# A two-layer kernel on one core: the skip term as transposes, B turned by four transposes, and another order of issue

## The chip, the cores and the metric

The kernel runs on one core of a Trainium2 chip. The metric is the device time of one execution in microseconds (us); lower is better. A core has a matrix engine (PE, whose weight loads the profile lists as PEld), three vector-like engines (DVE, ACT, POOL), and a queue, SP, that issues most of the DMAs.

## The reference

The input x is 16 images of 64 x 64 positions with 128 channels. Layer 0 normalises it in groups and runs a two-dimensional recurrence over the positions; its result is added to x. Layer 1 normalises that again and runs a state-space layer (Mamba) over the 4096 positions of an image, once forwards and once backwards with the same weights; the sum of both is added. The kernel spends most of its time in layer 1. What one direction computes, with 256 inner channels and 16 states:

```python
xz = x @ in_w.T
xc, z = jnp.split(xz, 2, axis=-1)
xt = conv(xc, conv_w)                       # 4 taps, causal, per channel
xc = silu(xt + conv_b)
dbl = xc @ x_w.T
dt, Bm, Cm = split(dbl, [8, 24], axis=-1)
dt = softplus(dt @ dt_w.T + dt_b)
A = -exp(A_log)
dA = exp(dt[..., None] * A)
dBx = dt[..., None] * Bm[:, :, None, :] * xc[..., None]
# for each position t:   h = dA_t * h + dBx_t;   y_t = sum over states of h * C_t
y = ys + xc * D
y = y * silu(z)
return y @ out_w.T
```

The change is about two places: `xc * D`, the skip term, and the way in which `Bm` reaches the product `dBx`.

## The kernel before

**Passes.** Layer 1 treats an image as 16 passes of 512 positions: passes 0 to 7 forwards, 8 to 15 backwards (`second` in the code). A pass holds two halves (h = 0 and 1) of 128 channels each, so a tile is 128 channels by 512 positions. There are 256 passes. During passes 0 and 1 of an image the next image is read as well, in eight pieces (`read_load`, `read_turn`, `read_take`, `read_stats`), and its group norm is worked out (`normal`). The tile for these loads, `xl`, exists once: a load waits until the piece before has been turned.

**One pass.** PE makes the convolution (`conv`, L1125), ACT `silu` of it, giving `xc`. PE projects it (`xproj`, L1162), and `dbl` holds the rows for dt, B and C. `dtproj` and `softplus` give `dt`; `times` on POOL gives `dtx` = dt * xc. For each of 16 states and both halves ACT makes `decay` (L1254), the tile `da` = exp(dt * A), and DVE runs a `scan` (L1308) over the positions: 32 scans a pass.

**States by two ways.** Four of the states (the units `0` and `1` of ORDER) get their input from POOL: `drive` (L1262) multiplies `dtx` with rows of B that were spread over the partitions (`br`). Their output is turned by PE (`turned`, L1340), taken by ACT (`turned_take`, L1348) and weighed with C on PE (`weigh`, L1355). The other twelve states (units `a` to `f`, four states each) get their input from PE: `drive_rows` (L1288) multiplies the transposed `dtx` (`turn`, L1242, and `turn_take`) with a matrix `d` that holds B on diagonals, and fills a quad of four PSUM banks (`hps`), which exists once. DVE scans from there; POOL multiplies two states with C (`out_of`, L1331, from `hst` and spread rows `cr` to `hc`), and PE adds them up with transposes into the output `py` (`sums`, L1368 through the helper `add`).

**The way of B.** `bturn` (L1182) turns `dbl` on PE, ACT takes it (`bturn_take`, L1193), SP writes it to a diagonal in DRAM (`scatter`, L1271, one DMA for four states), and loads the whole matrix from there (`spread`, L1207). The `scatter` of kind k does the same for C of the first four states straight from the rows in DRAM (L1278).

**Skip.** `ddiag` holds D on a diagonal, for each half. `skip` multiplies four blocks of `xc` with it on PE (L1368 through `add`), as the first contribution to `py`; `sums`, `weigh` and, backwards, `again` (the forward result, loaded by `recall`) add to it. Backwards follow `finish` on DVE, `back`, `back_take`, `project` and the store; `gate` and `gate_take` make silu(z) for that. Forwards, ACT's `finish` and a `spill` end the pass.

**The order.** Nothing in the kernel is ordered by hand. `order_of_issue` lists all operations with engine, dependences and buffers, and `simulate` plays them with assumed durations (COST, ISSUE, LINK) and an urgency for each kind of operation (URGENCY, a table for each direction); among the operations that are ready, the one with the lowest urgency is issued first. What comes out is the fixed order of instructions on each engine. RINGS gives the number of buffers of each kind; AHEAD and LEAD say how far the decays of the first four states may run ahead.

Of the kernel before, what the change touches and what calls it, by code (L numbers as in the profile page):

```python
# [8 lines left out]
F32 = mybir.dt.float32  # L9
# [5 lines left out]
P = 128  # L15
# [29 lines left out]
def units_of(order):  # L45

    count = {}
    for x in order:
# [4 lines left out]
        else:  # L53
# [6 lines left out]
    "br": 2, "cr": 6, "bt": 2, "xc": 5, "dt": 4, "dtx": 3, "dtxt": 3, "dbl": 2, "z": 1, "y": 1,  # L60
# [5 lines left out]
    "bturn": 0.5, "bturn_take": 0.23, "xproj": 1.0, "xproj_take": 0.4, "times": 1.2,  # L66
    "turn": 0.47, "turn_take": 0.555, "decay": 0.68, "drive": 2.4, "drive_rows": 1.13,
    "scan": 1.21, "keep": 0.6, "keep_group": 0.57, "out": 2.39, "sums": 0.88, "skip": 0.89,
# [3 lines left out]
    "read_take": 0.56, "read_stats": 0.69, "normal": 3.0, "normalise": 0.75, "spread": 0.6, "rows": 0.81,  # L72
# [10 lines left out]
AHEAD = 3  # L83
# [3 lines left out]
ISSUE = {"b": 0.7, "c": 0.7, "d": 0.51, "k": 0.45, "scatter_d": 0.82, "scatter_k": 1.77}  # L87
# [3 lines left out]
        {(0, 0): 226.07, (0, 1): 225.5, (0, 2): 209.71, (0, 3): 245.13, (1, 0): -224.93, (1, 1): -215.88,  # L91
         (1, 2): -217.49, (1, 3): -219.71},
        {(0, 0): 240.75, (0, 1): 97.67, (0, 2): 239.83, (0, 3): 183.31, (1, 0): -224.93, (1, 1): -236.77,
         (1, 2): -236.93, (1, 3): -239.63},
    ),
    "xproj": (
        {(): -4.49},
        {(): 88.92},
    ),
    "xproj_take": (  # L100
        {(): 12.43},
        {(): -21.38},
    ),
    "rows": (
        {(): -45.24},
        {(): -121.72},
    ),
    "bturn": (
        {(): 244.05},
        {(): -26.43},  # L110
    ),
    "bturn_take": (
        {(): 158.86},
        {(): 159.8},
    ),
    "dtproj": (
        {(0,): -250, (1,): -53.81},
        {(0,): 50.32, (1,): 50.35},
    ),
    "times": (  # L120
        {(0,): -65.05, (1,): -67.57},
        {(0,): 244.56, (1,): -165.67},
    ),
    "turn": (
        {(0,): 249.76, (1,): -134.89},
        {(0,): 229.21, (1,): 221.57},
    ),
    "turn_take": (
        {(0,): 47.45, (1,): 47.51},
        {(0,): 227.25, (1,): 226.2},  # L130
    ),
    "skip": (
        {(0,): 103.25, (1,): 218.48},
        {(0,): 89.87, (1,): 208.37},
    ),
    "spread": (
        {("b", 0): 48.09, ("d", 0): 223.16, ("c", 0): 189.13, ("c", 1): 239.27, ("d", 1): -105.98, ("c",
         2): 8.58, ("c", 3): 235.49, ("b", 1): 201.1, ("d", 2): 56.35, ("c", 4): 230.23, ("c", 5):
         215.44, ("k", 0): 139.69},
        {("b", 0): -14.32, ("d", 0): 47.86, ("c", 0): -35.94, ("c", 1): 138.92, ("d", 1): -107.61, ("c",  # L140
         2): -218.83, ("c", 3): -181.78, ("b", 1): -3.62, ("d", 2): 122.62, ("c", 4): 54.73, ("c", 5):
         240.7, ("k", 0): 139.45},
    ),
    "drive": (
        {(0, 0): -56.91, (1, 0): -57.77, (0, 1): 215.02, (1, 1): 247.85},
        {(0, 0): 171.33, (1, 0): 123.34, (0, 1): 160.79, (1, 1): 118.53},
    ),
    "decay": (
        {(0, 0): 224.88, (4, 0): 226.48, (5, 0): 240.06, (6, 0): 188.37, (7, 0): 250, (1, 0): 113.5, (8,
         0): 247.75, (9, 0): 250, (10, 0): 249.7, (11, 0): 249.33, (2, 0): 123.95, (12, 0): 249.4, (13,  # L150
         0): 176, (14, 0): 177.57, (15, 0): 243.29, (3, 0): 220.69, (4, 1): 238.79, (5, 1): 203.28, (6,
         1): 109.72, (7, 1): 15.19, (0, 1): 44.93, (8, 1): 223.62, (9, 1): 223.58, (10, 1): 225.51, (11,
         1): 223.77, (1, 1): 148.26, (12, 1): 223.35, (13, 1): 66.54, (14, 1): 65.52, (15, 1): 156.31,
         (2, 1): 205.76, (3, 1): 245.25},
        {(0, 0): 114.51, (4, 0): 225.16, (5, 0): 225.14, (6, 0): 226.99, (7, 0): 226.82, (1, 0): 116.2,
         (8, 0): 248.06, (9, 0): -17.84, (10, 0): -182.05, (11, 0): 70.11, (2, 0): 180.88, (12, 0):
         152.1, (13, 0): 166.91, (14, 0): 113.63, (15, 0): 222.06, (3, 0): 31.92, (4, 1): 221.8, (5, 1):
         236.29, (6, 1): 241.63, (7, 1): 222.65, (0, 1): 243.59, (8, 1): 198.45, (9, 1): 228.52, (10, 1):
         31.86, (11, 1): 26.36, (1, 1): 192.12, (12, 1): 244.33, (13, 1): 245.68, (14, 1): 241.41, (15,
         1): 243.62, (2, 1): 241.76, (3, 1): 250},  # L160
    ),
    "scan": (
        {(0, 0): -110.99, (4, 0): -110.09, (5, 0): -105.1, (6, 0): -105.34, (7, 0): -105.61, (1, 0):
         181.32, (8, 0): 19.6, (9, 0): 19.21, (10, 0): -80.71, (11, 0): 7.49, (2, 0): 40.13, (12, 0):
         -108.17, (13, 0): -102.34, (14, 0): -10.85, (15, 0): -108.25, (3, 0): -48.47, (4, 1): -48.83,
         (5, 1): -68.91, (6, 1): -83.82, (7, 1): -96.92, (0, 1): -31.74, (8, 1): -33.58, (9, 1): -38.05,
         (10, 1): -40.96, (11, 1): -50.07, (1, 1): 200.94, (12, 1): -50.19, (13, 1): -87.76, (14, 1):
         -88.26, (15, 1): -91.09, (2, 1): -5.51, (3, 1): -86.39},
        {(0, 0): -109.51, (4, 0): -109.17, (5, 0): -109.22, (6, 0): 181.52, (7, 0): 181.62, (1, 0):
         181.29, (8, 0): 178.29, (9, 0): 89.91, (10, 0): 53.07, (11, 0): 78.05, (2, 0): 236.4, (12, 0):  # L170
         238.58, (13, 0): 235.96, (14, 0): 231.8, (15, 0): 185.76, (3, 0): 215.03, (4, 1): -224.25, (5,
         1): -76.4, (6, 1): -164.06, (7, 1): -249.08, (0, 1): -59.15, (8, 1): 43.77, (9, 1): 17.69, (10,
         1): -44.01, (11, 1): 39.93, (1, 1): 179.06, (12, 1): 225.25, (13, 1): 220.27, (14, 1): 219.29,
         (15, 1): 208.64, (2, 1): 205.77, (3, 1): -93.1},
    ),
    "scatter": (
        {("d", 0): -144.33, ("d", 1): 131.97, ("d", 2): -55.93, ("k", 0): 242},
        {("d", 0): 229.49, ("d", 1): 250, ("d", 2): -140.49, ("k", 0): 202.88},
    ),
    "drive_rows": (  # L180
        {(0, 0): 146.61, (1, 0): 105.78, (2, 0): 191.69, (0, 1): 31.86, (1, 1): 23.35, (2, 1): 216},
        {(0, 0): 117.29, (1, 0): -235.5, (2, 0): -209.5, (0, 1): -218.03, (1, 1): -1.36, (2, 1): 220.27},
    ),
    "keep": (
        {(0, 0): 243.5, (1, 0): 34.18, (2, 0): 129.78, (3, 0): -79.15, (4, 0): 159.92, (5, 0): -249.25,
         (0, 1): 66.3, (1, 1): 176.21, (2, 1): 144.92, (3, 1): -209.94, (4, 1): 140.89, (5, 1): 96.84},
        {(0, 0): -158.59, (1, 0): 220.66, (2, 0): 74.58, (3, 0): -133.66, (4, 0): 174.52, (5, 0): 249.16,
         (0, 1): -179.84, (1, 1): -6.05, (2, 1): -230.81, (3, 1): -175.76, (4, 1): -72.61, (5, 1): 0.64},
    ),
    "out_of": (  # L190
        {(0, 0): 108.7, (1, 0): -34.28, (2, 0): -83.46, (3, 0): 208.24, (4, 0): 161.27, (5, 0): -58.6,
         (0, 1): 206.6, (1, 1): -49.46, (2, 1): -49.85, (3, 1): -249.28, (4, 1): -201.46, (5, 1): 30.29},
        {(0, 0): 70.5, (1, 0): -63.47, (2, 0): -69.72, (3, 0): 41.7, (4, 0): 117.41, (5, 0): 29.34, (0,
         1): -114.11, (1, 1): -106.56, (2, 1): -250, (3, 1): -250, (4, 1): -242, (5, 1): -12.92},
    ),
    "sums": (
        {(0, 0): 211.83, (1, 0): 214.79, (2, 0): 204.06, (3, 0): -118.64, (4, 0): 34.31, (5, 0): -162.93,
         (0, 1): 232.47, (1, 1): 221.1, (2, 1): 203.91, (3, 1): 184.07, (4, 1): -222.45, (5, 1): -216.44},
        {(0, 0): -193.31, (1, 0): -194.97, (2, 0): -209.87, (3, 0): -189.32, (4, 0): -201.67, (5, 0):
         -91.54, (0, 1): 250, (1, 1): 236.49, (2, 1): 104.24, (3, 1): 225.82, (4, 1): 240.77, (5, 1):  # L200
         166.95},
    ),
    "keep_group": (
        {(0, 0): 208.79, (0, 1): -155.94},
        {(0, 0): -223.05, (0, 1): -200.24},
    ),
    "turned": (
        {(0, 0, 0): -242.59, (0, 0, 1): 198.86, (0, 0, 2): -19.69, (0, 0, 3): -164.84, (0, 1, 0): 211.89,
         (0, 1, 1): -221.33, (0, 1, 2): -221.83, (0, 1, 3): -131.66},
        {(0, 0, 0): -224.04, (0, 0, 1): 147.65, (0, 0, 2): -245.55, (0, 0, 3): -163.35, (0, 1, 0):  # L210
         142.63, (0, 1, 1): 126.52, (0, 1, 2): 128.31, (0, 1, 3): 130.7},
    ),
    "turned_take": (
        {(0, 0, 0): 63.6, (0, 0, 1): 44.72, (0, 0, 2): 65.41, (0, 0, 3): 65.32, (0, 1, 0): -184.53, (0,
         1, 1): 128.22, (0, 1, 2): 127.61, (0, 1, 3): 106.49},
        {(0, 0, 0): 55.23, (0, 0, 1): 9.13, (0, 0, 2): 192.65, (0, 0, 3): 192.3, (0, 1, 0): -181.41, (0,
         1, 1): -222.89, (0, 1, 2): 132.46, (0, 1, 3): 131.21},
    ),
    "weigh": (
        {(0, 0): -231.65, (0, 1): -206.75},  # L220
        {(0, 0): -4.68, (0, 1): 4.67},
    ),
# [1276 lines left out]
```

## Time and profile before

| | |
|---|---|
| median of three runs | 12566.69 us (12562.89 to 12603.51) |
| the profiled execution | 12569.44 us, span 12567.3 us |
| mean granted clock of PE | 0.992 |
| busy: PE, DVE, POOL, ACT | 96%, 89%, 84%, 79% |
| POOL `hc` (out_of) | 7384.9 us in 3072 instructions, 2431 ns each |
| DVE `hst` scans with carry | 6466.2 us in 5376, 1261 ns each |
| ACT `da` (decay) | 5404.7 us in 8192, 710 ns each |
| PE `py<-ddiag,xc` (skip) | 580.2 us in 4096 records, 285 ns each |

Busy time is that in which an engine has at least one instruction under way. PE's instructions overlap, so the mean duration of one is longer than the distance from one to the next; what an operation on PE costs is read from the start of the next one. The profile names an operation by its line and its tiles, out<-in. "Idle before" gives the time for which the engine stood and what it waited for. The first pass of layer 1 begins 1538 us into the span.

### The profile page before, as it was taken

How to read it: one execution, taken by the hardware profiler on the slowest of the kernel's cores; microseconds unless marked ns; L12 is line 12 of the kernel's file. 1: busy time of each engine (PE TensorE's matmuls, PEld its weight loads, DVE VectorE, ACT ScalarE, POOL GpSimd, SP SyncE). 2: the span in 40 equal slices, each digit the busy share in tenths (PEclk: the TensorE clock that was granted, in tenths of full speed). 3: DMA queues.
4: the chain of work that ended last, by engine and by line, in shares of the span. 5: the costliest groups of instructions: out<-in, count | busy, mean ns of one | idle time of the engine just before them, and what ended most of it. 6: DMA issues, size and time to landing. Idle time of an engine off the chain costs nothing. (4 is left out here: it accounts for less than half of the span.)

```text
span 12567.3 us, 322625 instructions
## 1 busy us (share of the span) xinstructions
PE 12114.5 (96%) x128820; PEld 9486.8 (75%) x128820; DVE 11138.3 (89%) x11409; ACT 9954.8 (79%) x15936; POOL 10578.2 (84%) x4868
## 2 busy tenths in 40 slices
PE   9999999999999999999999999999999999999999
PEld 8656877777777777777777777777777777777777
DVE  7767699998989999999999998999999999999998
ACT  3444588888888888888888888888888888888887
POOL 0111299999999999999999999999999999999998
PEclk9999899999999999999999999999999999999999
DMA  4222255555556555555555555555555555556564
GB/s 156 56 56 56 64 162 160 158 166 158 160 157 166 159 160 158 165 160 158 167 159 162 158 163 161 162 163 158 162 158 163 159 163 161 162 159 165 158 164 140
DMA packets 2320782, 1885.92 MB, mean 150 GB/s; under 512 B 1537696, under 2 KB 1883312, under 8 KB 2319280
## 3 DMA queue, kind: packets, MB, share of 16 engines
q1 hardware_dynamic: 2241328, 1830.04, 52.2%
q10 hardware_dynamic: 77952, 35.24, 1.2%
q8 instruction: 1017, 16.66, 0.5%
q14 instruction: 485, 3.97, 0.1%
HBM read 1698.25 MB, written 164.30 MB: 148 GB/s over the span
## 5 line engine op out<-in xcount | busy, mean ns | idle before, releaser
L1331 POOL TENSOR_TENSOR hc<-hst,cr 128x1024 f32<-128x1024 f32 x3072 | 7384.9, 2431 | 465.0 <-DVE hst L1308 307.3
L1308 DVE TENSOR_TENSOR_SCAN hst<-da,carry,hps 128x512 f32<-128x512 f32 x5376 | 6466.2, 1261 | 535.0 <-issue 219.7
L1254 ACT ACTIVATE da<-dt,A_log_sb 128x512 f32<-128x512 f32 x8192 | 5404.7, 710 | 843.3 <-DVE hst L1308 783.9
L1368 PEld LDWEIGHTS py<-ident,hc 128*128 128x128 f32 x24576 | 2763.6, 142 | 769.0 <-issue 358.3
L1368 PE MATMUL py<-ident,hc 128*128 128x128 f32 x24576 | 3108.0, 275 | 165.7 <-POOL hc L1331 154.5
L1262 POOL TENSOR_TENSOR group<-dtx,br 128x1024 f32<-128x1024 f32 x1024 | 2447.0, 2403 | 134.8 <-PE ptg L1340 85.8
L1308 DVE TENSOR_TENSOR_SCAN group<-da,carry,group 128x512 f32<-128x512 f32 x1792 | 2243.8, 1266 | 118.9 <-ACT da L1254 108.3
L1288 PEld LDWEIGHTS hps<-d,dtxt 32*128 32x128 f32 x49152 | 1526.0, 187 | 621.8 <-issue 280.3
L1125 PE MATMUL pp<-xT,wk 128*128 128x512 f32 x4096 | 1954.8, 599 | 1.7 <-ACT dt L1229 1.2
L1288 PE MATMUL hps<-d,dtxt 32*128 32x128 f32 x49152 | 1810.0, 283 | 139.4 <-DVE hst L1308 117.3
L1348 ACT COPY ht<-ptg 128x512 f32<-128x512 f32 x2048 | 1126.9, 588 | 430.6 <-PE ptg L1340 398.9
L887 POOL TENSOR_TENSOR a_f<-a_f,c 128x16 f32<-128x16 f32 (+35 forms) x254 | 188.6, 743 | 1313.9 <-ACT a_f L879 1250.2
L1340 PE MATMUL ptg<-ident,group 128*128 128x128 f32 x8192 | 1153.0, 278 | 35.4 <-DVE group L1308 18.5
L1340 PEld LDWEIGHTS ptg<-ident,group 128*128 128x128 f32 x8192 | 922.4, 142 | 256.9 <-issue 91.9
L1125 PEld LDWEIGHTS pp<-xT,wk 128*128 128x128 f32 x4096 | 697.5, 190 | 524.9 <-issue 496.1
L1308 DVE TENSOR_TENSOR_SCAN hst<-da,hps 128x512 f32<-128x512 f32 x768 | 874.6, 1199 | 83.8 <-PE hps L1288 46.4
L1235 POOL TENSOR_TENSOR dtx<-dt,xc 128x512 f32<-128x512 f32 x512 | 646.8, 1288 | 61.6 <-DMA d<-d 29.5
L1254 ACT ACT_TABLE_LOAD x527 | 676.1, 1283 | 9.4
L1368 PE MATMUL py<-ddiag,xc 128*128 128x128 f32 x4096 | 580.2, 285 | 13.3 <-ACT y L1415 10.8
L1355 PE MATMUL py<-ht,k 128*32 128x128 f32 x16384 | 559.8, 277 | 2.6 <-ACT ht L1348 1.2
L879 ACT ACTIVATE a_f<-pg_f,b_sb 128x16 f32<-128x16 f32 (+35 forms) x508 | 219.7, 472 | 415.2 <-DMA x<-xl 212.7
L1368 PEld LDWEIGHTS py<-ddiag,xc 128*128 128x128 f32 x4096 | 496.2, 191 | 59.3 <-ACT y L1415 25.4
(113 smaller groups left out, 12431.2 us busy)
## 6 DMA issues: line engine op xcount, KB each, us to landing
cr<-rows SPq DMA_DIRECT2D x1536, 512.0 KB
d<-d SPq DMA_DIRECT2D x768, 448.0 KB
br<-rows SPq DMA_DIRECT2D x512, 512.0 KB
k<-k SPq DMA_DIRECT2D x256, 256.0 KB
yf<-y SPq DMA_DIRECT2D x128, 512.0 KB
yl<-yf SPq DMA_DIRECT2D x128, 512.0 KB
carry<-hst SPq DMA_DIRECT2D x3072, 1.0 KB
xs<-in_x_dram SPq DMA_DIRECT2D x64, 512.0 KB
```

The source lines that it names most:

```text
L879: nc.scalar.activation(agv.rearrange("p i b -> p (i b)"), pgv, AF.Tanh if g == "c" else AF.Sigmoid, bias=b_sb[:, gi : gi + 1],)
L1125: nc.tensor.matmul(self.ps["conv", h], lhsT=wk[:, k, h * P : (h + 1) * P], rhs=xT[self.b % 2][:, t0 : t0 + T], start=(k == 0), stop=(k == ...
L1235: nc.gpsimd.tensor_mul(self.dtx[h], self.dt[h], self.xc[h])
L1254: nc.scalar.activation(t, self.dt[h], AF.Exp, scale=amat[:, h, s : s + 1])
L1262: nc.gpsimd.tensor_mul(both[:, m : m + 2, :], bc(self.dtx[h], 1, 2), self.brow[q])
L1288: nc.tensor.matmul(part[:, j, :, :], lhsT=self.dtxt[h][rows, j, :], rhs=dg[rows, j + r, :, :], start=True, stop=True, skip_group_check=True,)
L1308: nc.vector.tensor_tensor_scan(t[:, self.rev], self.da.pop((s, h))[:, self.rev], dbx[:, self.rev], 0.0 if self.first else carry[:, self.d, ...
L1331: nc.gpsimd.tensor_mul(self.hc[g, h], self.hst[g, h].rearrange("p t m -> p m t"), self.crow[g])
L1340: nc.tensor.transpose(pt[:, k, :], self.group[g, h][:, t0 : t0 + TB, :].rearrange("p t s -> p (t s)"), ident,)
L1348: nc.scalar.copy(t, self.ps.pop(("turned", g, h, j)))
L1355: nc.tensor.matmul(self.py[h][q * TB : (q + 1) * TB, j * P : (j + 1) * P], lhsT=cd[:, GX * j + q, :], rhs=self.ht[g, h, j][:, q, :], start ...
L1368: nc.tensor.matmul(self.py[h][:, cols], **{"start": False, "stop": False, **how}, skip_group_check=True)
```

## The change

It does four things.

- `skip` no longer multiplies with `ddiag`. A new operation `scaled` on ACT multiplies `xc` by D (a factor for each partition), into a new tile `xd` with two buffers, and `skip` adds `xd` to `py` by four transposes. `ddiag` goes.
- `bturn` uses four transposes of all 128 partitions onto 64, in place of eight matmuls of 64x64; `bturn_take` copies 96 elements on 64 partitions instead of 48 on 128. The two halves of the positions lie side by side then, and `scatter` of kind d writes each by a DMA of its own: two issues for four states instead of one.
- `dtx` has two buffers instead of three.
- COST, ISSUE, AHEAD and the whole table URGENCY have other values, so the order of instructions on every engine is another one. The order of the scans on DVE stays the same but for the finishes and statistics between them.

```diff
-    "br": 2, "cr": 6, "bt": 2, "xc": 5, "dt": 4, "dtx": 3, "dtxt": 3, ...
+    "br": 2, "cr": 6, "bt": 2, "xc": 5, "xd": 2, "dt": 4, "dtx": 2, "dtxt": 3, ...
...
-AHEAD = 3
+AHEAD = 0
...
-ISSUE = {"b": 0.7, "c": 0.7, "d": 0.51, "k": 0.45, "scatter_d": 0.82, "scatter_k": 1.77}
+ISSUE = {"b": 0.45, "c": 0.44, "d": 0.46, "k": 0.34, "scatter_d": 1.2, "scatter_k": 0.65}
...
         for h in range(NH):
-            put("skip", (h,), "PE", after=[("silu", i, h)], takes=[py[h]], uses=[T_["xc"][h]], chain=("skip", 0))
+            xd = tile_of("xd")
+            put("scaled", (h,), "ACT", after=[("silu", i, h)], takes=[xd], uses=[T_["xc"][h]], chain=("scaled", 0))
+            put("skip", (h,), "PE", after=[get(("scaled", i, h))], takes=[py[h]], uses=[xd, T_["xc"][h]], chain=("skip", 0))
...
-            for h in range(NH):
-                nc.vector.tensor_scalar_mul(ddiag[:, h, :], ident, dvec[:, h, :])
...
-                pt = self.ps["bturn"] = bank(place, f"pbt_{self.nm}", (P, NB, QP))
+                pt = self.ps["bturn"] = bank(place, f"pbt_{self.nm}", (QP, NB, P))
                 strided = self.dbl.rearrange("p (i j) -> p j i", j=NB)
                 for j in range(NB):
-                    for q in range(NQ):
-                        part = slice(q * QP, (q + 1) * QP)
-                        nc.tensor.matmul(
-                            pt[part, j, :],
-                            lhsT=strided[part, j, :],
-                            rhs=ident[part, part],
-                            ...
-                        )
+                    nc.tensor.transpose(pt[:, j, :], strided[:, j, :], ident)
...
             def bturn_take(self):
-                self.bt = ring(cp, "bt", [P, NB, NS - NX], f"bt_{self.nm}")
-                nc.scalar.copy(self.bt, self.ps.pop("bturn")[:, :, RANK + NX : RANK + NS])
+                self.bt = ring(cp, "bt", [QP, NB, NQ, NS - NX], f"bt_{self.nm}")
+                pt = self.ps.pop("bturn").rearrange("p j (q s) -> p j q s", q=NQ)
+                nc.scalar.copy(self.bt, pt[:, :, :, RANK + NX : RANK + NS])
...
                 if kind == "d":
-                    dst = bass.AP(t.tensor, t.offset, [[WD + GX, P], [P, NB], [1, GX]])
-                    nc.sync.dma_start(dst, self.bt[:, :, GX * g : GX * (g + 1)])
+                    for q in range(NQ):
+                        dst = bass.AP(
+                            t.tensor, t.offset + q * QP * (WD + GX), [[WD + GX, QP], [P, NB], [1, GX]]
+                        )
+                        nc.sync.dma_start(dst, self.bt[:, :, q, GX * g : GX * (g + 1)])
                     return
...
+            def scaled(self, h):
+                self.xd[h] = ring(cp, "xd", [P, T], f"xd_{self.nm}_{h}")
+                nc.scalar.activation(self.xd[h], self.xc[h], AF.Copy, scale=dvec[:, h, :])
+
             def skip(self, h):
 
                 for j in range(NB):
                     self.add(
                         h,
                         slice(j * P, (j + 1) * P),
-                        lhsT=self.xc[h][:, j * P : (j + 1) * P],
-                        rhs=ddiag[:, h, :],
+                        lhsT=self.xd[h][:, j * P : (j + 1) * P],
+                        rhs=ident,
+                        is_transpose=True,
                     )
```

What the new order does at the places that matter below, told from the two programs' instructions. In pass 1 of an image, read_turn(4) on PE stood between the last `turned` and the `weigh` of the pass before; now it stands behind `drive_rows(2,0)`, and read_turn(3), (5), (6) and (7) lie between other operations than they did. The three small matmuls of `normal` stood ahead of that pass's `drive_rows(2,1)` and now stand behind it. In passes 3 to 7, `times(1)` and `turn(1)`, issued in the pass before until now, come in the pass itself, after its third scan. On SP, in passes 3 to 7, the issue behind the scatter of kind k is the spread of the next pass's first `cr`; before, it was mostly a `keep` or a d scatter.

## The prediction

> **What bounds the kernel now.** I read the page's busy shares first. They do not decide: four engines are above 79%.
>
> ```profile
> PE 12114.5 (96%) x128820; PEld 9486.8 (75%) x128820; DVE 11138.3 (89%) x11409; ACT 9954.8 (79%) x15936; POOL 10578.2 (84%) x4868
> ```
>
> So I cut the seventh image (counting from 0) at the first scan of each of its sixteen passes, in the view of busy time by window. The columns are the window, its length, then busy us and instructions of PE, PEld, DVE, ACT and POOL, the granted clock, the DMA share and GB/s. The passes shown are 0, 1, 2, 5, 8, 10 and 11.
>
> ```profile
> 6363.20:6408.50 45.30, 44.30 (x498) 34.85 (x498) 39.57 (x38) 39.65 (x62) 42.71 (x20) 1.00 0.55 160
> 6408.50:6460.10 51.60, 46.30 (x489) 38.00 (x487) 42.42 (x43) 43.17 (x68) 42.01 (x19) 0.90 0.64 173
> 6460.10:6500.30 40.20, 37.61 (x456) 29.23 (x449) 38.12 (x32) 36.99 (x58) 35.85 (x17) 1.00 0.48 133
> ...
> 6581.50:6622.20 40.70, 38.55 (x457) 30.12 (x456) 38.09 (x34) 34.71 (x54) 40.54 (x19) 1.00 0.59 156
> ...
> 6704.10:6746.30 42.20, 40.41 (x469) 31.96 (x468) 37.29 (x35) 33.54 (x53) 41.94 (x19) 1.00 0.62 172
> ...
> 6790.40:6834.10 43.70, 43.66 (x493) 34.89 (x492) 40.38 (x37) 36.36 (x58) 40.68 (x19) 1.00 0.57 159
> 6834.10:6877.80 43.70, 43.66 (x493) 34.88 (x492) 40.35 (x37) 36.34 (x58) 40.69 (x19) 1.00 0.57 164
> ```
>
> Three regimes show. In passes 9 to 15 PE is busy 43.66 of 43.70 us while every other engine idles 3 us or more: PE alone sets the time. In passes 3 to 8 POOL is busy all but 0.2 to 0.4 us of about 41: POOL sets it. Passes 0 and 1 hold the next image's reading; pass 1 leaves every engine idle for 5 us or more and has a clock of 0.90.
>
> Next the timeline of PE in such a PE-bound pass (start, length, engine, line, what).
>
> ```profile
> 6263.12 1.17 PE L1182 MATMUL pbt<-ident,dbl 64*64 64x64 f32 x16
> 6264.22 0.75 PE L1242 MATMUL ptx<-ident,dtx 128*128 128x128 f32 x4
> 6264.90 1.08 PE L1355 MATMUL py<-ht,k 128*32 128x128 f32 x32
> ...
> 6267.69 1.16 PE L1368 MATMUL py<-ddiag,xc 128*128 128x128 f32 x8
> 6268.69 0.60 PE L1423 MATMUL pb<-ident,y 128*128 128x128 f32 x4
> 6269.13 1.04 PE L1368 MATMUL py<-ident,hc 128*128 128x128 f32 x8
> ```
>
> No wait stands at any line, and an operation costs the distance to the next start: bturn 1.10 us, this skip 1.00, four plain transposes (pb) 0.44. The records also show that a matmul is two records and a transpose one: skip's four make x8, bturn's eight x16, pb's four x4. Last, the same view in pass 1:
>
> ```profile
> 6415.47 0.63 PE L1049 MATMUL pt<-ident,xl 128*128 128x128 f32 x4 [1.83 <-DMA xl<-x]
> 6416.03 1.57 PE L1355 MATMUL py<-ht,k 128*32 128x128 f32 x32
> 6417.53 2.09 PE L1288 MATMUL hps<-d,dtxt 32*128 32x128 f32 x32
> ...
> 6447.63 0.56 PE L736 MATMUL pm_l<-mv,gavg 128*128 128x1 f32 x2
> 6448.12 2.09 PE L1288 MATMUL hps<-d,dtxt 32*128 32x128 f32 x32
> ```
>
> Here a read_turn waits for its load, and drive_rows (hps) runs 2.09 us instead of 1.17 behind it; later it stands behind the three matmuls of the group norm.
>
> **The change on PE.** Skip: in that pass the first takes 0.89 us (start 6240.73 to 6241.62) and the second 1.00, together 1.89. The new ones are four transposes each with the same shape as pb and ptg, which take 0.44 (pb above) to 0.50 (pb from 6240.23 to 6240.73). Two cost 0.88 to 1.00, so 0.89 to 1.01 goes; I take 0.95. Bturn: four transposes read with a stride, onto 64 partitions. No row shows that. The nearest are pb's 0.44 and turn's 0.68 (ptx, strided, twice the columns). Against 1.10 that saves 0.42 to 0.66; I take 0.55, nearer the plain one because each load is half turn's. Together 1.31 to 1.67 us a pass, taken as 1.50: PE's need in passes 9 to 15 falls from 43.66 to 42.16.
>
> **Does the time follow?** POOL's 40.7 us there leaves room. DVE is tighter. Each quad of PSUM is freed by a scan, refilled by PE and read again, so DVE has idle time that it can't avoid. Pass 2 shows how much: neither POOL (idle 4.35) nor PE (2.59) is the bound there, and DVE idles 40.20 − 38.12 = 2.08. With DVE's 40.35 this gives 42.43, just above PE's 42.16. I take 42.5, from 43.76 on the mean of passes 9 to 15: 1.25 × 7 × 16 images = 140 us. The bounds are 1.6 (PE's whole saving, 180 us) and 0.75 (hand-offs worse than in pass 2, 84 us). Passes 2 to 8 are POOL's or the hand-off's: nothing.
>
> **Passes 0 and 1.** Pass 0 is PE's too (44.30 of 45.30): 1.2 us × 15 images = 18. In pass 1 the new order puts read_turn(4) behind weigh, two drive_rows, skip, two sums and four conv after read_turn(3): about 1.0 + 2.2 + 0.5 + 1.7 + 3.4 = 8.8 us of PE work. The load needed 4.95 from issue (6410.52 on SP) to use, so the 1.83 and the 0.24 wait before it go. The group norm's three matmuls now follow drive_rows(2,1); before, that one was free to start at 6446.0 and started at 6448.1: 2.1 us. With PE's own 1.5 that is 5.7. But between read_turn(4) and (5), and (6) and (7), stand only some 4.7 and 4.1 us of PE work against 4.95: I give back 2.2. ACT, busy 43.17 of 51.6, keeps room. 3.5 × 15 = 52 us; bounds 0 and 5.7 × 15 = 86.
>
> **What is added.** Two scaled activations of 128x512 on ACT: 11 decays of that size take 6.85 us in a row, 0.62 each, so 1.24; skip, which now waits for ACT, comes about 30 scans behind its scaled, for both h. ACT goes from 36.3 to 37.6 of 42.5, and its 5 us of idle hide them; what is queued behind one is a decay, whose tiles are up to 9 ahead. If that cover were gone, 1.24 × 7 × 16 = 139 us would come back. bturn_take grows from 48 to 96 elements: 0.20 us to at most the 0.37 of dbl's 256; take 0.03, hidden likewise. The dtx ring of 2 moves times(1) and turn(1) of passes 3 to 7 behind the pass's third scan; they are needed at drive(0,1) and drive_rows(0,1), some ten scans later, so nothing waits. ddiag's two products at the start: under 1 us.
>
> Each d scatter becomes two issues on SP: 3 more a pass, 0.50 us each (the median of the old ones), 1.5 us beside some 20 us of issuing in 43. What is queued behind them is the cr and d spreads, which are used ten us and more after their issue, and the keeps, which the next pass needs: nothing; the other bound is the 3.4 us which the issue behind k's scatter takes now, 3 × 3.4 a pass, still under SP's waiting. [...]
>
> **Sum.** 140 + 18 + 52 = 210 us. The profiled execution took 12569.4 (span 12567.3), 2.7 above the median of three runs, 12566.7. So 12569.4 − 210 = 12359, or 12356 beside the median.
>
> **Rivals.** (1) The hand-offs hold more than pass 2 shows, 43.0 a pass, and pass 1 gains nothing: 84 + 18 = 102, 12,465. For it: PE, DVE and POOL are then within 2 us of each other. Against: pass 2's row. 0.11.
>
> (2) More: passes 9 to 15 reach PE's 42.16 (180), and pass 1 gains all (86 + 22 in pass 0): 12,280. For it: PE waits 0.04 us a pass now. 0.07.
>
> (3) Half clock. Transposes replace matmuls, and if they keep the clock up less, PE slows in the passes which it sets. One spell like those in pass 1 costs about 2 us (2.09 − 1.17 for drive_rows, as much again in its neighbours); one in every PE-bound pass is 2 × 7 × 16 = 224: 12,580, no change. Against: passes 9 to 15 are full of transposes and show 1.00. [...] 0.05.
>
> (4) Slower: the SP queue starves POOL. Behind k's scatter the next issue takes about 3.4 us on SP (138 d scatters stood there, median 3.38). In passes 3 to 7 the new order puts a cr spread there, and three more issues follow. POOL multiplies with cr, and in passes 2 to 8 each us it waits is lost. It decides from 1.9 us of POOL waiting in each (250 / (8 × 16)); with the full 3.4 in eight passes, 3.4 × 128 = 435 − 210 = 225 slower, 12,790. For it: POOL waited 52.5 us for cr in 8000 before, so the margin isn't endless. Against: in the trace its buffer comes free 28.9 us into the pass and is first used 7.4 us into the next, some 19 us later. 0.11.
>
> **Numbers.** The forecast, 12,300 to 12,430, has 0.66. The range 12,240 to 12,520 takes in rivals 1 and 2 as well (0.84). About 0.3%, 38 us, is what a measurement of this kernel can tell from no change. Faster: 0.66 + 0.11 + 0.07 = 0.84, less a little for a rival 1 that falls shorter, 0.82; same 0.06; slower 0.12.
>
> **What would show it.** Right: windows of passes 9 to 15 at 42.2 to 42.9 with PE idle under 0.8, skip's start distances at 0.44 to 0.50, bturn's at 0.44 to 0.68, passes 3 to 8 unchanged with POOL idle under 0.8, pass 1 without a wait of 1.8 on xl before weigh. Wrong: a PE wait on ACT xd, POOL waits on cr in passes 3 to 8, a clock below 1.00 in passes 9 to 15, or PE's need above 42.5.

## The result, and the profile after

The changed kernel took 12487.88 us (median of four runs, 12473.08 to 12499.37) against 12577.49 for the kernel before in the same comparison: a ratio of 0.9926, with a 95% interval of 0.9903 to 0.9949. It is faster by 0.7%, where the prediction said 1.7%. The profiled execution took 12473.08 us, its span 12471.1.

The busy shares of the page again decide nothing:

```profile
PE 11816.2 (95%) x123700; PEld 9141.1 (73%) x123700; DVE 11102.2 (89%) x11407; ACT 10217.3 (82%) x16448; POOL 10573.6 (85%) x4868
```

Busy time by window, cut at the first scan of each pass of the seventh image, as before (window, length, then PE, PEld, DVE, ACT and POOL busy, granted clock, DMA share, GB/s). Shown are passes 0, 1, 2, 3, 5, 8 and 11:

```profile
6322.80:6365.60 42.80, 41.47 (x481) 33.17 (x480) 39.64 (x39) 38.75 (x63) 42.68 (x20) 1.00 0.60 171
6365.60:6415.40 49.80, 43.04 (x474) 33.95 (x473) 42.13 (x42) 45.37 (x72) 42.48 (x19) 0.95 0.66 183
6415.40:6456.90 41.50, 36.52 (x421) 28.04 (x420) 38.18 (x32) 38.34 (x60) 37.65 (x17) 0.95 0.50 130
6456.90:6501.10 44.20, 38.11 (x438) 29.83 (x439) 38.16 (x33) 35.76 (x56) 41.72 (x19) 0.96 0.49 148
...
6543.20:6584.80 41.60, 37.95 (x444) 29.19 (x444) 38.14 (x34) 35.79 (x56) 40.04 (x19) 1.00 0.58 161
...
6666.70:6707.70 41.00, 37.91 (x438) 29.00 (x436) 36.98 (x35) 33.72 (x53) 40.10 (x19) 1.00 0.54 159
...
6793.10:6835.50 42.40, 42.40 (x477) 33.32 (x473) 39.98 (x37) 37.40 (x59) 40.67 (x19) 1.00 0.56 165
```

The PE-bound pass 11 is 1.3 us shorter, with PE busy for all of it. But pass 3 has 44.20 us in which no engine is busy for more than 41.72, and the clock is 0.95 to 0.96 in passes 2 and 3. Pass 3 of before had a clock of 1.00, and POOL was busy for nearly all of it:

```profile
6500.30:6541.40 41.10, 38.92 (x458) 30.29 (x458) 38.21 (x33) 34.78 (x54) 40.92 (x19) 1.00 0.57 155
```

One image is too few to judge by, so here is each pass as a mean over images 1 to 15 (the distance from the first scan of a pass to the first of the next, read from the traces):

| pass | before | after | change |
|---|---|---|---|
| 0 | 45.26 | 42.65 | −2.61 |
| 1 | 49.63 | 49.03 | −0.60 |
| 2, 3, 4, 5 | 40.43, 41.04, 40.93, 40.91 | 42.11, 42.58, 42.54, 42.76 | +1.68, +1.54, +1.61, +1.85 |
| 6, 7, 8 | 41.20, 41.24, 41.79 | 41.31, 40.22, 41.54 | +0.11, −1.02, −0.25 |
| 9 to 15, mean | 43.76 | 42.46 | −1.30 |

Passes 9 to 15 give 1.30 × 7 × 16 = 146 us, and passes 2 to 6 take back 6.79 × 16 = 109. Passes 0, 1, 7 and 8 together give 4.48 × 16 = 72, about the 70 that was forecast for passes 0 and 1. So passes 2 to 6 are where the missing gain went.

Where PE is the bound, its timeline shows the new operations at their forecast pitch: bturn (`pbt`) 0.57 us to the next start, skip (`xd`) 0.44.

```profile
6824.16 0.64 PE L1182 MATMUL pbt<-ident,dbl 128*64 128x128 f32 x4
6824.73 0.72 PE L1236 MATMUL ptx<-ident,dtx 128*128 128x128 f32 x4
...
6828.66 0.60 PE L1365 MATMUL py<-ident,xd 128*128 128x128 f32 x4
6829.10 1.15 PE L1365 MATMUL py<-ident,hc 128*128 128x128 f32 x9
```

Now the lost time, in pass 3. The timeline of DVE, with the idle time before a group and its releaser in brackets:

```profile
6490.20 2.45 DVE L1305 TENSOR_TENSOR_SCAN hst<-da,carry,hps 128x512 f32<-128x512 f32 x2 [0.17 <-issue]
6496.41 2.45 DVE L1305 TENSOR_TENSOR_SCAN hst<-da,carry,hps 128x512 f32<-128x512 f32 x2 [3.76 <-DMA carry<-hst]
```

The scan that starts at 6496.41 is scan(14,1). It writes an `hst` buffer, of which there are three, and the DMA carry<-hst that it waits for is keep(2,1), which still reads the buffer that it needs. The timeline of SP's queue says why this 1 KB arrives so late:

```profile
6483.82 0.60 SPq L1275 DMA_DIRECT2D k<-rows  x1
6484.51 1.33 SPq L1207 DMA_DIRECT2D cr<-rows  x1
6485.93 0.38 SPq L1201 DMA_DIRECT2D d<-d  x1
6486.41 0.38 SPq L1207 DMA_DIRECT2D cr<-rows  x1
6486.91 2.25 SPq L1317 DMA_DIRECT2D carry<-hst  x1
```

The keep is the fifth issue, behind the scatter of kind k and three loads of 512, 448 and 512 KB for the next pass. It is issued at 6486.91 and the scan is released at 6496.41, 9.5 us later. In pass 3 of before only two loads, of 448 and 512 KB, stood ahead of it:

```profile
6526.42 1.01 SPq L1198 DMA_DIRECT2D rows<-dbl  x2
6527.52 0.37 SPq L1207 DMA_DIRECT2D d<-d  x1
6528.99 0.34 SPq L1213 DMA_DIRECT2D cr<-rows  x1
6529.44 0.59 SPq L1278 DMA_DIRECT2D k<-rows  x1
6530.11 3.79 SPq L1320 DMA_DIRECT2D carry<-hst  x1
```

On the mean of passes 3 to 5 the keep is issued 0.4 to 0.5 us after the scan whose result it copies, so it isn't issued late; it lands late, 7.9 to 8.1 us after its issue, where before it was 5.8 to 6.0 (from the landing events of the traces).

While DVE waits, PE has no quad to read or refill, and it starts again at about half its speed. The granted clock is 1.00 over the 2.74 us of matmuls ahead of the wait, 0.56 over the 1.92 us of drive_rows behind it and 0.54 over the 1.95 us of sums after that:

```profile
6491.81 2.74 PE L1127 MATMUL pp<-xT,wk 128*128 128x512 f32 x6
6498.97 1.92 PE L1285 MATMUL hps<-d,dtxt 32*128 32x128 f32 x32 [4.41 <-issue]
6500.82 1.95 PE L1365 MATMUL py<-ident,hc 128*128 128x128 f32 x8
```

This is no accident of one pass. DVE's idle time before scan(14,1), averaged over the images, is 1.92, 2.49, 2.35 and 2.57 us in passes 2 to 5, over 1 us in all 16 images of each; before it was 0.17 to 0.42. In these passes all three loads stand ahead of the keep. In pass 6, with two loads and a d scatter ahead of it, it is 1.00, and in pass 7, with two loads and no d scatter, 0.08. In 8000 us (from 3000 to 11000), the list of waits has DVE's wait on carry<-hst (total, times, longest), before and after:

```profile
DVE hst L1308 <- DMA carry<-hst: 40.9, 65, 1.9
DVE hst L1305 <- DMA carry<-hst: 119.1, 73, 4.0
```

### The profile page after: what moved, and what is told of

Read it like the earlier page. It is cut to its first block, busy times and chain, and to the rows that moved or that the text cites. A ratio compares the mean times of both kernels' runs of the same rounds, so it can differ in the third digit from the quotient of the medians.

```text
span 12471.1 us, 314271 instructions
## 1 busy us (share of the span) xinstructions
PE 11816.2 (95%) x123700; PEld 9141.1 (73%) x123700; DVE 11102.2 (89%) x11407; ACT 10217.3 (82%) x16448; POOL 10573.6 (85%) x4868
## 5 line engine op out<-in xcount | busy, mean ns | idle before, releaser
L1365 PE MATMUL py<-ident,hc 128*128 128x128 f32 x24576 | 3207.3, 277 | 31.8 <-POOL hc L1328 30.9
L1365 PEld LDWEIGHTS py<-ident,hc 128*128 128x128 f32 x24576 | 2812.4, 143 | 516.2 <-issue 346.6
L1285 PE MATMUL hps<-d,dtxt 32*128 32x128 f32 x49152 | 1835.7, 286 | 395.6 <-issue 237.0
L1337 PE MATMUL ptg<-ident,group 128*128 128x128 f32 x8192 | 1193.6, 281 | 59.8 <-ACT ht L1345 33.8
L1213 PE MATMUL pv<-dbl,dt_wT 128*128 128x256 f32 x2048 | 531.4, 392 | 0.0
L1352 PEld LDWEIGHTS py<-ht,k 128*32 128x32 f32 x16384 | 414.0, 110 | 112.0 <-issue 43.2
```

What stands on the lines that cost most here:

```text
L1213: nc.tensor.matmul(pv[:, q * TQ : (q + 1) * TQ], lhsT=dt_wT[:, q, h * P : (h + 1) * P], rhs=self.dbl, start=True, stop=True,)
L1285: nc.tensor.matmul(part[:, j, :, :], lhsT=self.dtxt[h][rows, j, :], rhs=dg[rows, j + r, :, :], start=True, stop=True, skip_group_check=True,)
L1337: nc.tensor.transpose(pt[:, k, :], self.group[g, h][:, t0 : t0 + TB, :].rearrange("p t s -> p (t s)"), ident,)
L1352: nc.tensor.matmul(self.py[h][q * TB : (q + 1) * TB, j * P : (j + 1) * P], lhsT=cd[:, GX * j + q, :], rhs=self.ht[g, h, j][:, q, :], start ...
L1365: nc.tensor.matmul(self.py[h][:, cols], **{"start": False, "stop": False, **how}, skip_group_check=True)
```

## The experiments

Three theories stand. The **keep theory**: the new order puts three loads ahead of keep(2,1), and DVE's wait for the buffer sets passes 2 to 6. The **clock theory**: PE, with less work, falls to half clock, and that costs the time. The **code theory**: the doubled scatters, or scaled on ACT, cost it in any order. Each experiment is compared with the kernel before on its own chip; that kernel took 12,573 us on one chip, 12,649 and 12,652 on a second and 12,620 on a third, so ratios are compared.

**The keep moved.** SP's order in passes 2 to 7, here that of pass 3:

```diff
   scatter+2(k,0)
+  keep(2,1)
   spread+1(c,0)
   spread+1(d,1)
   spread+1(c,1)
-  keep(2,1)
   scatter+2(d,2)
```

> The kernel after, with one thing moved: in passes 2 to 7 the keep of (2,1), the small DMA carry<-hst, is issued ahead of the next pass's loads cr(c,0), d(d,1) and cr(c,1) instead of behind them. Nothing is computed otherwise. Keep theory: scan(14,1) waits for a free hst buffer, which that keep still reads, because the keep lands behind three 0.5 MB loads; so the wait of about 2 us per pass (DVE hst <- DMA carry<-hst, 119 us in the stretch 3000:11000) falls to below 40 us, passes 2 to 5 go from 42.1-42.8 back to 41.0-41.5 us, and the whole is shorter by 70 to 110 us: 12,380 to 12,420 us. Clock theory (PE has less work, so it is granted half clock and that is what costs) and code theory (two scatters, scaled on ScalarE): no change, 12,470 to 12,505 us.

Measured: 12336.13 us, ratio 0.9809 (0.9795 to 0.9822). Passes 2 to 6 are at 40.26, 40.49, 40.35, 40.49 and 40.67. The same pass 3 in its timelines of SP's queue and of DVE:

```profile
6425.16 0.48 SPq L1340 DMA_DIRECT2D carry<-hst  x1
6425.73 0.54 SPq L1230 DMA_DIRECT2D cr<-rows  x1
6426.36 0.38 SPq L1224 DMA_DIRECT2D d<-d  x1
6426.87 0.35 SPq L1230 DMA_DIRECT2D cr<-rows  x1
```

```profile
6428.82 4.80 DVE L1328 TENSOR_TENSOR_SCAN hst<-da,carry,hps 128x512 f32<-128x512 f32 x4 [0.17 <-issue]
```

The keep goes out first, and scans (12,1) to (15,1) run as one group of four with no wait inside. On the mean of passes 3 to 5 the keep lands 1.9 to 2.2 us after its issue. In the same 8000 us DVE waits for carry<-hst for 28.1 us, none of it before scan(14,1) in passes 2 to 7:

```profile
DVE hst L1328 <- DMA carry<-hst: 28.1, 41, 2.5
```

The window of this pass shows what sets it now:

```profile
6395.70:6435.90 40.20, 36.68 (x437) 28.26 (x436) 38.18 (x34) 35.89 (x56) 40.20 (x19) 1.00 0.54 152
```

POOL is busy for all of it. The doubled scatters and scaled are all still there, so the code theory falls for the new order; the keep's place is what costs. The effect was larger than expected, 152 us instead of 70 to 110: with no load ahead of the keep, passes 2 to 7 also come out 0.2 to 0.7 us below those of before, 3.0 × 16 = 48 us per run. It is also the fastest version of the study but for one that leaves work out.

**The wait filled.** In passes 2 to 5, ahead of drive_rows(0,0) of the next pass:

```diff
+  conv_more+3(0,0) conv_more+3(0,1) conv_more+3(0,2) conv_more+3(0,3)
   drive_rows+1(0,0)
```

> The kernel after; in passes 2 to 5 the four matmuls conv(0,.) of the third next pass are made a second time, with the same result, ahead of the next pass's drive_rows(0,0), where TensorE stands for up to 4.4 us: 1.8 us of work put into the wait. Clock theory (what costs is that TensorE falls to half clock in that wait, and drive_rows and sums behind it take 1.9 us for 1.2 and 1.0): the passes 2 to 5 get 0.9 to 1.5 us shorter, the whole 12,395 to 12,440 us. Keep theory (VectorE's wait for the hst buffer sets the pass, the half clock only follows from it): passes 2 to 5 within 0.5 us of 42.1 to 42.8, the whole 12,465 to 12,515 us.

Measured: 12525.15 us, ratio 0.9903 (0.9889 to 0.9916), an interval that overlaps that of the changed kernel. Passes 2 to 5 take 42.56, 42.68, 42.67 and 42.77. Its timelines of PE and of DVE at the end of a pass 3:

```profile
6527.23 3.60 PE L1155 MATMUL pp<-xT,wk 128*128 128x512 f32 x8
6530.76 1.17 PE L1313 MATMUL hps<-d,dtxt 32*128 32x128 f32 x32
```

```profile
6527.85 2.45 DVE L1333 TENSOR_TENSOR_SCAN hst<-da,carry,hps 128x512 f32<-128x512 f32 x2 [2.66 <-DMA carry<-hst]
```

The added matmuls, 3.6 us at the pitch shown and not the 1.8 that the expectation said, keep drive_rows at 1.17 us, and the granted clock of this pass is 1.00. DVE's wait is still there, and the passes are as long as the keep theory expected.

But that expectation took its 42.1 to 42.8 us from a comparison in which the kernel before took 12,577 us; on the chip of this run it took 12,649. On that same chip ran a kernel, told of below, that differs from the changed one in pass 1 alone (its group norm is taken apart). Its passes 2 to 5 take 42.23, 43.38, 43.59 and 43.67 us. DVE's idle time before scan(14,1) is the same in both: 2.92, 2.85 and 3.08 us in passes 3 to 5 there, 2.98, 2.96 and 3.10 with the wait filled. Against that kernel, filling the wait made passes 3 to 5 shorter by 0.7 to 0.9 us, and pass 2 longer by 0.3.

So the clock theory is half right. Half clock follows from the wait, and most of the loss is the wait, which the filling leaves in place. But half clock has a price of its own. In the trace of the changed kernel the first drive_rows behind the wait took over 1.5 us in 23 of the 64 passes 2 to 5, and 1.17 in 36. From scan(14,1) to scan(12,1) of the next pass it is 38.2 us behind a slow one and 37.3 behind one of 1.17 (passes 3 to 5); the next wait is then 0.5 us shorter, so 0.5 to 1.0 us is lost. At 23 passes that is 12 to 23 us of the 109, an estimate. The length of PE's gap alone doesn't tell which it will be: the 23 slow ones stood behind gaps of 2.0 to 4.5 us, the 36 at full speed behind gaps of 1.2 to 3.8.

**The new order with the old code.** Only the functions are exchanged:

```diff
-  (after) scaled, skip by transposes, bturn by four transposes, two scatters
+  (before) skip against diag(D), bturn by eight matmuls, one scatter
```

> The order of the kernel after with the code of before: skip against diag(D), two turns, one scatter, and scaled left out. Nothing is computed otherwise. Keep theory (order): passes 2 to 5 stay at 42.1 to 42.8 us or longer, passes 9 to 15 go back to 43.8 us; 12,488 plus 16 x 7 x 1.32 gives 12,636 us (12,600 to 12,660), slower than before. Code theory: passes 2 to 6 come back to 41 us, 12,636 less 108 gives 12,530 us (12,510 to 12,560).

Measured: 12737.21 us, ratio 1.0132 (1.0118 to 1.0146). Passes 2 to 5 are at 42.5 to 43.2, and DVE idles 1.4 to 2.3 us before scan(14,1). So the loss comes with the order, without the new code, as the keep theory has it. It is larger than the 60 us expected, 164: 131 are in passes 2 to 5, whose excess over before is 8.2 us an image, and 33 in passes 9 to 15, which take 44.05.

**The new code with the old order**, at first with one buffer for xd, for want of room:

```diff
-    ... "xc": 5, "dt": 4, "dtx": 3, ...
+    ... "xc": 5, "xd": 1, "dt": 4, "dtx": 3, ...
...
+  scaled+1(0) behind decay(2,1) and skip(1); scaled+1(1) behind skip+1(0)
```

> The changed code (skip from scaled x, four turns, two scatters) issued in the order of the kernel before, with scaled(i,h) put in behind the last decay of the pass before; the ring xd has one buffer for want of room. Nothing is computed otherwise. Keep theory (the order costs the time, not the code): passes 2 to 8 stay at 40.4 to 41.8 us as before, passes 9 to 15 fall from 43.76 to about 42.5 us, passes 0 and 1 stay at 45.3 and 49.6 us; 12,577 less 16 x 7 x 1.3 gives 12,430 us (12,410 to 12,450). Code theory: passes 2 to 6 lengthen by 6.7 us per image with this order too, so 12,540 us (12,520 to 12,560).

Measured: 12769.81 us, ratio 1.0153 (1.0134 to 1.0172), far from both expectations. With one buffer ACT must stand until skip has read it; the list of waits has

```profile
ACT xd L1397 <- PE py L1380: 225.1, 178, 3.1
```

which makes this run no test of the question. It was made again with the rings of the kernel after:

```diff
-    ... "xd": 1, "dt": 4, "dtx": 3, ...
+    ... "xd": 2, "dt": 4, "dtx": 2, ...
...
-  scaled+1(0) behind decay(2,1) and skip(1); scaled+1(1) behind skip+1(0)
+  scaled+1(0) behind decay(2,0) and skip(0); scaled+1(1) behind decay(2,1) and skip(1)
```

> As e2_code_old_order, the changed code in exactly the order of before with scaled put in, but with the rings of the kernel after: xd of two buffers and dtx of two in place of three, so that ScalarE no longer stands for the skip that reads xd (225 us of such waits in 8 ms of e2_code_old_order). Nothing is computed otherwise. If the order is what cost the time in the forward passes: passes 2 to 8 at 40.4 to 41.8 us, passes 9 to 15 at 42.5 us, a ratio to before of 0.987 to 0.990. If the changed code costs time whatever the order: passes 2 to 6 or 9 to 15 above those of before, a ratio of 0.996 or more.

Measured: 12751.80 us, ratio 1.0109 (1.0095 to 1.0123): a miss for the keep theory as I had put it. Passes 3 to 7 take 42.2 to 42.8 and passes 9 to 13 about 44.1, with PE busy for 42.5 to 42.7 of them. DVE's list of waits for the buffer:

```profile
DVE hst L1320 <- DMA carry<-hst: 200.2, 171, 4.5
```

The wait is the same, in other places: before scan(14,1) DVE idles 0.75 us in passes 3 to 7, and before scan(6,0), which needs the buffer that keep(4,1) of the pass before reads, 1.72 us in passes 9 to 13 (0.21 before). In the old order keep(4,1) stands behind all d scatters, and there are twice as many now. The place given to scaled and the two buffers of dtx are part of this run too; no run separates them.

**The scatters moved out of the way**, in that last kernel, in every pass:

```diff
-  scatter+2(...)   (the four between keep(1,1) and keep(5,1))
   keep(2,1) ... keep(4,1) keep(5,1)
+  scatter+2(...)   (all four, in their order)
   spread+1(c,3)
```

> e2b_code_old_order (the changed code in the order of before, ratio 1.011) with the scatters of two passes on moved on SyncE behind keep(5,1), so that keep(2,1) and keep(4,1) no longer stand behind them. Nothing is computed otherwise. If it is the doubled scatters ahead of the keeps that cost the time in e2b_code_old_order (scan(14,1) waits 0.6 us in passes 3 to 5 and scan(6,0) 1.8 us in passes 9 to 13 for an hst buffer): passes 9 to 13 from 44.1 to about 42.5 us, passes 3 to 7 from 42.4 to 41.5 us or less, a ratio to before of 0.988 to 0.997. If it is something else in the changed code under that order: passes 9 to 13 within 0.5 us of 44.1 us, a ratio of 1.005 or more.

Measured: 13303.51 us, ratio 1.0519 (1.0505 to 1.0533): much slower. What was to go has gone: the mean idle time before scan(14,1) and scan(6,0) is nil in passes 3 to 7 and 9 to 13. But the scatters now stand ahead of keep_group(0,1) and cr(c,3), and POOL's drive waits for the first:

```profile
POOL group L1289 <- DMA carry<-group: 523.1, 151, 9.4
```

(74.5 us in the kernel with the scatters in their old place.) DVE passes it on as 4.1 us before scan(10,0) in passes 3 to 7. Passes 9 to 13 do not fall to 42.5 but take 44.2 to 44.9, as scan(10,0) there waits 1.5 us, put down to another keep. So it is shown that the scatters delay whatever stands behind them on SP, and that the two waits came from scatters ahead of the keeps. It isn't shown what the new code would take in the old order with no keep delayed, since this version delays another one.

**One scatter in the new order:**

```diff
-  (after) bturn by four transposes onto 64 partitions, two scatters for four states
+  (before) bturn onto 128 partitions, one scatter for four states
```

> The kernel after with the turn of B and its scatter as before: two turns onto 128 partitions, one scatter for four states. Nothing is computed otherwise. Keep theory: passes 2 to 5 stay at 42 to 43 us, passes 9 to 15 lengthen by the 0.55 us that the new turn saved on TensorE, to 43.0; 12,488 plus 16 x 7 x 0.55 gives 12,550 us (12,530 to 12,570). Scatter theory (the second scatter on the queue is what makes the keep late): passes 2 to 5 come back to 41 us, 12,550 less 16 x 5.5 gives 12,460 us (12,440 to 12,480).

Measured: 12664.71 us, ratio 1.0015 (1.0007 to 1.0024), 0.9% above the changed kernel's ratio, and 0.7% above that of the kernel on the same chip with the group norm taken apart. Passes 9 to 15 take 43.1, 0.7 more, near the 0.55 expected. Passes 2 to 5 don't come back: 42.3 to 43.9, against 42.2 to 43.7 in that kernel on the same chip, with DVE idle for 2.2 to 3.3 us before scan(14,1). In the new order it isn't the second scatter that delays keep(2,1): in these passes no d scatter stands between keep(1,1) and that keep.

**Pass 1.** Its group norm, `normal`, was put ahead of drive_rows(2,1) again, where before had it:

```diff
+  normal-15()
   drive_rows(2,1)
   scaled+1(1)
-  normal-15()
```

> The kernel after, with the group norm of the next image (normal) put ahead of drive_rows(2,1) in pass 1, where the order of before had it. Nothing is computed otherwise. Order theory for pass 1: VectorE no longer waits 1.6 us for pm behind drive_rows(2,1); pass 1 goes from 49.0 to between 47 and 48 us, the whole to 12,455 to 12,475 us. Rival (pass 1 is set by ScalarE, busy for 45 of its 49 us, and by the two function table loads): pass 1 stays within 0.4 us of 49.0 us, the whole at 12,480 to 12,495 us. Passes 2 to 6 are not touched: still 42 to 43 us.

Measured: 12487.60 us, ratio 0.9927 (0.9914 to 0.9939), pass 1 at 49.03, to the digit that of the changed kernel. Next the group norm was taken apart, its six steps put between other work:

```diff
-  normal-15()
+  read_stats-15(7) norm_sum ... conv+3(0,3) norm_mean ... scan(1,1) norm_dev ...
+  turn+1(1) norm_var ... turn_take+1(1) norm_std ... scan(12,1) norm_scale
```

> The kernel after with the group norm taken apart alone, the keep not moved. If the waits of VectorE in the group norm set pass 1: 12,440 to 12,465 us; if not: 12,475 to 12,500 us. Passes 2 to 6 stay at 42 to 43 us either way.

> The keep moved as in e1_keep (12,336 us), and in pass 1 the group norm of the next image taken apart into its steps, each put between scans and matmuls that have their data, so that VectorE no longer stands for pm and std (1.8 + 1.8 us in one pass 1 of the kernel after). Nothing is computed otherwise. If these waits set pass 1: 49.0 to 46-47.5 us, the whole at 12,291 to 12,311 us. If ScalarE sets it (busy 45 of 49 us, two table loads among it): pass 1 within 0.4 us of 49.0, the whole at 12,330 to 12,342 us.

Measured: 12569.15, ratio 0.9944 (0.9931 to 0.9957), for the first and 12412.51, ratio 0.9818 (0.9804 to 0.9831), for the second: no gain over 0.9926 and 0.9809. Pass 1 takes 50.7 and 50.6 us in the two, and 50.0 in the kernel with the wait filled, whose pass 1 is that of the changed kernel, on the same chip. Then ACT's square root was moved to DVE, to rid ACT of two table loads (1.28 us each, one before the square root and one before the next decay in the changed kernel's trace), on top of the moved keep:

```diff
-        nc.scalar.activation(std, pv, AF.Sqrt, bias=eps)
-        ...
+        nc.vector.tensor_scalar_add(var, pv, GN_EPS)
+        nc.vector.tensor_scalar(std, var, 0.5, 0.5, ALU.mult, ALU.add)
+        for _ in range(4):
+            nc.vector.reciprocal(scale, std)
+            nc.vector.scalar_tensor_tensor(std, scale, var, std, ALU.mult, ALU.add)
+            nc.vector.tensor_scalar_mul(std, std, 0.5)
+        nc.vector.reciprocal(scale, std)
```

> e1_keep (ratio 0.981), with the square root of pass 1's group norm worked out on VectorE (four steps of Heron's rule, 14 small instructions of 0.16 us) in place of ScalarE's Sqrt, whose function table costs ScalarE two loads of 1.28 us in pass 1. The result agrees to rounding. If ScalarE sets the end of pass 1: pass 1 from 49.1 to 46.5-47.5 us, a ratio of 0.977 to 0.979. If VectorE's own chain sets it: pass 1 at 49 us or longer by up to 1 us, a ratio of 0.981 to 0.983.

Measured: 12399.81, ratio 0.9825 (0.9812 to 0.9839), pass 1 at 50.3. ACT is busy 2.3 us less in pass 1 than with the moved keep alone and DVE 2.2 more. The ratio shows no gain over 0.9809; no run on this chip has the moved keep alone, so its pass 1 can't be compared directly. Last, the whole computation was left out:

```diff
+            if b >= 2:
+                norm[b] = norm[1]
+                return
```

> e1_keep, without the group norm's own computation from the third image on: its mean, deviation, square root and the two table loads are left out and the scale and shift of the second image taken for all (so the output differs); the reading, the statistics and the normalise stay. It bounds what this computation costs pass 1. If it sets the end of pass 1 (4.3 us of VectorE's time, 2.6 us of ScalarE's): pass 1 at 45 to 46 us, a ratio of 0.976 to 0.978. If pass 1 is long for its other work (statistics on VectorE, takes and normalise on ScalarE): 48 us or more, a ratio of 0.980.

Measured: 12340.03, ratio 0.9780 (0.9766 to 0.9793), pass 1 at 46.6, 3.7 us less than with the square root on DVE on the same chip. So the computation, a chain from DVE over PE and ACT and back, is worth at most about that (the version with the square root on DVE is the longer one on DVE), and neither another place for it nor relief of ACT is seen to recover any of it. Even without it pass 1 has 4.6 to 5.4 us of idle time on each of the four engines; what sets the rest stays open.

## Why the prediction was off

**Passes 9 to 15: the number right, in part by luck.** Forecast 42.5, measured 42.46; skip at a pitch of 0.48 us on the mean of all passes (forecast 0.44 to 0.50) and bturn at 0.59 (0.44 to 0.68). In passes 9 to 15 the two saved 0.95 and 0.54 us a pass, as forecast. But the stop at 42.5 was argued from DVE's idle time, and PE is busy without a gap: its need was 0.3 above the forecast 42.16. The sum left out what the new order does to PE's other work. dtproj's matmuls take 2.03 us a pass instead of 1.88 and gate's 1.83 instead of 1.73, and in the run of the new order with the old code they take the same 2.03 and 1.82. That this ends at the same 42.5 is luck.

**Pass 0: right in sign, too small.** It gave 2.6 us an image instead of 1.2; why it gave more was not examined.

**Passes 2 to 8: wrong, and the step that decided.** "Passes 2 to 8 are POOL's or the hand-off's: nothing" cost 109 us in passes 2 to 6. The failing step is the sentence on SP's queue: "and the keeps, which the next pass needs: nothing". It asked who reads what a keep writes, and found the next pass. It didn't ask what the keep reads: an hst buffer, one of three, which scan(14,1) of the same pass must have back. DVE's wait for it grew to 1.9 to 2.6 us in passes 2 to 5, with PE's half clock behind it. With the buffer freed by moving one DMA, the time is 12,336, 20 us below the forecast. That this is so near is partly cancellation: pass 1 fell some 40 us short of its 52, while passes 2 to 7 gave 48 that nobody forecast and pass 0 some 20 more than its 18. The list of signs held POOL's waits on cr, which fell (52.5 us to 16.3), and ACT's xd, on which PE has no wait of note; DVE's wait on carry<-hst wasn't on it, though the list of waits of before showed it with 40.9 us.

**Pass 1: 0.6 us instead of 3.5.** The wait on xl before weigh has gone, and by scan(15,0) pass 1 is 3.8 us ahead of before (18.3 us into it instead of 22.1). By scan(3,0) only 0.8 is left, as two statistics, one of which waits 1.35 us for its read_turn, stand between the two now. The second term, 2.1 us for drive_rows(2,1) no longer behind the group norm, is refuted by the run that put it back: 49.03 either way. What sets the rest of pass 1 stays open.

**What the doubled scatter costs.** The prediction gave the second issue nothing in its sum. In the new order that was right for passes 2 to 5, which were no shorter with one scatter. In the old one it was not: 1.72 us before scan(6,0) in passes 9 to 13, the wait for a small DMA that is queued behind the scatters.

**The rivals.** Rival 4 had the right queue and the wrong transfer: cr had room to spare, the keep had none. Rival 1's 12,465 is nearest to the result, but by another sum: of its two conditions, pass 1 without a gain came and 43.0 us in passes 9 to 15 did not. Rival 3 is refuted for the PE-bound passes (clock 1.00 in pass 11). Half clock did come in passes 2 to 5, behind DVE's wait and not for the transposes, at the 12 to 23 us estimated above.

## What to carry to other kernels

A DMA out of a buffer has two users waiting for it: whoever reads the copy, and whoever needs the buffer back. When an order of issue is changed, list for every small store the ring it frees, and count the bytes that now stand ahead of it on its queue (1472 KB here, and DVE stood 1.9 to 2.6 us for the buffer). A change of code and a change of order can each lose alone (here 1.1% and 1.3%) and gain together, so neither is judged without the other; and moving a burst of issues away from one victim can choose the next, as it did here with the scatters (1.0519).

## What the runs showed of the hardware

- A DMA of 1 KB, issued behind loads of 512, 448 and 512 KB on the same queue, released its waiter 9.5 us after its issue began. On the mean of passes 3 to 5 the keep landed 7.9 to 8.1 us after its issue behind three loads, 5.8 to 6.0 behind the two of before, and 1.9 to 2.2 ahead of them, where it held nobody up.
- PE ran at about half speed behind a gap of 4.41 us (drive_rows 1.92 us instead of 1.17, at a granted clock of 0.56; eight transposes 1.95 instead of 1.09, at 0.54). Kept busy through such gaps, it stayed at a granted clock of 1.00 in passes 3 to 5 of the seventh image, and passes 3 to 5 on the mean were 0.7 to 0.9 us shorter than on the same chip without it, DVE's wait being the same.
- Passes 10 to 13 took the same on different chips (42.4 us with the moved keep on one, 42.3 to 42.5 with the group norm taken apart on another), while passes 3 to 5 of the latter kernel took 43.4 to 43.7 there, against 42.3 to 43.0 on the first chip for the one with `normal` put first; both differ from the changed kernel only in pass 1. The keep landed 8.5 to 8.7 us after its issue there, against 7.7 to 8.3 on the first chip, and drive_rows behind the wait was slow more often (30 of 64 passes 2 to 5, against 22). So part of it is how late a queued DMA lands; why chips differ in that, no run shows.
